# A message-passing layer on one core: the gather of B[dst] and the scatter of edge sums replaced by 0/1 matmuls over a window of 64 nodes

## The chip, the cores and the metric

The kernel runs on one core of a Trainium2 chip. The metric is device time in microseconds (us) of one launch. The program is the same for every run, and its inputs are fixed by a seed.

## The reference

There are N = 6250 nodes with 128 features and E = 100000 edges with 4 attributes. The edges are **sorted by destination**; on average a node has 16 of them.

```python
# x: [6250, 128], src, dst: [100000] (sorted by dst), edge_attr: [100000, 4]
msg_in = concat([x[src], x[dst], edge_attr], axis=1)      # [E, 260]
h = silu(msg_in @ mW1 + mb1)
messages = h @ mW2 + mb2
aggregated = segment_sum(messages, dst, num_segments=N)
u = silu(concat([x, aggregated], axis=1) @ uW1 + ub1)
y = layer_norm(x + u @ uW2 + ub2, ln_g, ln_b)
out = layernorm(x + y)
```

## The kernel before

The linear parts of the edge network are moved to the nodes. With A = x @ mW1a and B = x @ mW1b + mb1, an edge needs silu(A[src] + B[dst] + edge_attr @ mW1e). The second matrix is applied after the sums, because sum(h @ mW2 + mb2) = sum(h) @ mW2 + degree * mb2. All arithmetic is in float32.

The work has three stages.

**Tables (lines 94 to 195).** Nodes lie on 128 partitions, 49 to each. x is loaded, transposed on TensorE in batches of four node tiles, and multiplied to A and B. Both go to tables in DRAM, `tab_a` and `tab_b` (lines 194, 195). Two accumulators in DRAM, `acc`, are filled with zeros by two large DMAs on ScalarE's queue (line 170). ScalarE's queue also issues the weight loads, among them 16 small ones for the block-diagonal edge weights `we` (line 121).

**Edges (lines 198 to 307).** 128 edges make a tile, 4 tiles a group, and there are 196 groups, so 784 tiles. For each tile GpSimd (POOL) issues three indirect DMAs: a gather of A[src] into `ga`, one of B[dst] into `gb` (both line 229), and a scatter that adds 128 rows of 144 numbers to an accumulator (line 292). Gathers run 3 groups ahead. A group's computing is: transposes of the destinations (`pd`, line 254), a 0/1 matrix of equal destinations within a tile (`same`, line 256), three further VectorE operations that find which lane comes first (lines 260 to 268), the edge attributes' part (`pre`, line 272), two additions (lines 276, 277), silu on ScalarE (`h`, line 279), four products of `same` with `h` (`ph`, line 285) and two copies out of PSUM (line 288).

**Node update and the norms (lines 309 to 422).** Per batch of four node tiles, both accumulators are loaded (line 328) and added (line 330), transposed (`ps_s`, `ps_d`, lines 334, 335) and sent through the update network: `ps_a` (343, 344), `ps_u` (349, 352), silu (354), `ps_y` (358). Then the two norms follow in chunks of 7 node tiles (lines 392 to 422).

The order on each engine is not the program's order. A scheduler that runs when the kernel is built places an operation on its engine as soon as its inputs and a free buffer are there by its own reckoning; the buffer counts (`bufs`) bound how far it runs ahead. On each engine the order is then fixed, and semaphores carry the waits.

Of the kernel before, what the change touches and what calls it, by code (L numbers as in the profile page):

```python
# [12 lines left out]
AX = mybir.AxisListType  # L13
PSUM = bass.MemoryType.PSUM
DRAM = bass.MemoryType.DRAM

P = 128
EPS = 1e-5


@with_exitstack
def kernel(
# [30 lines left out]
    """  # L53
# [5 lines left out]
    NP = P * NT  # L59
    G = 4                       # edge tiles in a group  # L60
    C = 16                      # edge tiles whose attributes are transposed together
    ET = -(-E // (P * C)) * C
    NG = ET // G
    W = 144                     # features, degree, and zeros up to a multiple of 64 bytes
    K = 2                       # accumulators that scatters alternate between
    SPARE = NP                  # first spare row
    NA = NP + P
    AHEAD = 3                   # groups that gathers run ahead
# [4 lines left out]
    def load_rows(tile_, src_rows, n_rows, per, split=112):  # L73
        """Rows p * per .. of a [n_rows, ...] array to partition p; the last partition may be short."""
        full = n_rows // per
        for p0, p1 in ((0, min(split, full)), (min(split, full), full)):
            if p1 > p0:
                nc.sync.dma_start(
                    tile_[p0:p1],
                    src_rows[p0 * per : p1 * per].rearrange("(p j) c -> p j c", j=per),  # L80
                )
        rest = n_rows - full * per
        if rest:
            nc.sync.dma_start(
                tile_[full : full + 1, :rest],
                src_rows[full * per : n_rows].rearrange("(p j) c -> p j c", p=1),
            )
# [7 lines left out]
    x_sb = consts.tile([P, NT, H], F32, name="x_sb")  # L95
    last = N // NT
    if N % P or N % NT:
        nc.vector.memset(x_sb[96:P], 0.0)
    load_rows(x_sb, x, N, NT)
# [4 lines left out]

    src_i = consts.tile([P, ET, 1], I32, name="src_i")
    dst_i = consts.tile([P, ET, 1], I32, name="dst_i")
    ea = consts.tile([P, ET, ED], F32, name="ea")
    nc.gpsimd.memset(src_i[96:P], 0)
    nc.gpsimd.memset(dst_i[96:P], N)
    nc.gpsimd.memset(ea[96:P], 0.0)  # L110
    load_rows(src_i, src.rearrange("(e o) -> e o", o=1), E, ET)
    load_rows(dst_i, dst.rearrange("(e o) -> e o", o=1), E, ET)
    load_rows(ea, edge_attr, E, ET)

    # block-diagonal edge weights: row (j, c) holds mW1e[c] in block j
    NB = C // G
    we = consts.tile([C * ED, NB, G * H], F32, name="we")
    nc.vector.memset(we, 0.0)
    for j in range(C):
        b, g = divmod(j, G)  # L120
        nc.scalar.dma_start(we[j * ED : (j + 1) * ED, b, g * H : (g + 1) * H], mW1[2 * H :])

# [15 lines left out]
    ident = consts.tile([P, P], F32, name="ident")  # L138
    make_identity(nc, ident)
    col = consts.tile([P, P], I32, name="col")  # L140
    nc.gpsimd.iota(col, pattern=[[1, P]], base=0, channel_multiplier=-1)
    below = consts.tile([P, P], F32, name="below")      # column < partition
    nc.vector.tensor_scalar(below, col, 0.0, None, op0=OP.is_lt)
    spare_i = consts.tile([P, 1], I32, name="spare_i")
    nc.gpsimd.iota(spare_i, pattern=[[0, 1]], base=SPARE, channel_multiplier=1)
    spare = consts.tile([P, 1], F32, name="spare")
    nc.vector.tensor_copy(spare, spare_i)
# [4 lines left out]
    tab_a = dram.tile([NP, H], F32, name="tab_a")  # L152
    tab_b = dram.tile([NP, H], F32, name="tab_b")
    acc = [dram.tile([NA, W], F32, name=f"acc{k}") for k in range(K)]
    xT = consts.tile([P, NT * P], F32, name="xT")

    def by_node(t):
        return t[:NP].rearrange("(p i) f -> p i f", i=NT)

    def groups(n, g):  # L160
        return [(i, min(g, n - i)) for i in range(0, n, g)]

    with tc.tile_pool(name="tables", bufs=3) as work, tc.tile_pool(
        name="zero", bufs=1
    ) as zpool, tc.tile_pool(name="tables_ps", bufs=2, space=PSUM) as ps:
        NZ = NA * W // P
        zeros = zpool.tile([P, NZ], F32, name="zeros")
        nc.gpsimd.memset(zeros, 0.0)
# [29 lines left out]
    with ExitStack() as edges:  # L198
        idxp = edges.enter_context(tc.tile_pool(name="idxp", bufs=1))
        gath = edges.enter_context(tc.tile_pool(name="gath", bufs=AHEAD + 2))  # L200
# [4 lines left out]
        dst_f = idxp.tile([P, ET], F32, name="dst_f")  # L205
        nc.vector.tensor_copy(dst_f, dst_i.rearrange("p j o -> p (j o)"))
        to_spare = idxp.tile([P, ET], F32, name="to_spare")
        nc.vector.tensor_scalar(to_spare, dst_f, -1.0, spare, op0=OP.mult, op1=OP.add)
        NH = 3
        hbuf = []  # L210
        for i in range(NH):
            h = idxp.tile([P, G, W], F32, name=f"h{i}")
            nc.vector.memset(h[:, :, H:], 0.0)
            nc.vector.memset(h[:, :, H : H + 1], 1.0)
            hbuf.append(h)

        rows = {}

        def gather(g, i):
            if g >= NG:  # L220
                return
            if i == 0:
                rows[g] = (
                    gath.tile([P, G, H], F32, name="ga"),
                    gath.tile([P, G, H], F32, name="gb"),
                )
            j = g * G + i
            for t, tab, idx in zip(rows[g], (tab_a, tab_b), (src_i, dst_i)):
                nc.gpsimd.indirect_dma_start(  # L229
                    out=t[:, i, :],  # L230
                    out_offset=None,
                    in_=tab[:, :],
                    in_offset=bass.IndirectOffsetOnAxis(ap=idx[:, j, :], axis=0),
                )
# [221 lines left out]
```

## Time and profile before

| | |
|---|---|
| Time, median of 3 runs | 3765.49 us (3764.08 to 3770.97) |
| Profiled execution, first to last instruction (span) | 3770.8 us |
| First gather starts | 80.92 us |
| Last scatter starts | 3613.53 us |
| Mean granted TensorE clock | 0.523 of full speed |

No time is listed for the profiled execution apart from its span; the span lies 5.3 us over the median and 0.2 us under the slowest of the three runs, so that span and time are read as one here.

How to read the profile: the engines are PE (TensorE's matmuls), PEld (its weight loads, which overlap PE), DVE (VectorE), ACT (ScalarE), POOL (GpSimd) and SP (SyncE, which only issues DMAs here). A name with q (SPq) is an engine's instruction queue. "out<-in" names tiles of the program. In the timeline the columns are start in us, duration in us, engine, line, operation, tiles, shapes, count, and in brackets the engine's idle time before it and what ended it. A float32 matmul appears as two rows (784 of them at line 285 make x1568), a transpose as one.

### The profile page before, as it was taken

The numbers are of one execution on the slowest core, as the hardware profiler recorded it, in microseconds if no ns is written. First come the engines' busy times: TensorE is split into PE (matmuls) and PEld (weight loads), VectorE is DVE, ScalarE is ACT, GpSimd is POOL, SyncE is SP. The second block draws the span as 40 slices with busy tenths as digits, with TensorE's granted clock in tenths as the row PEclk, the third lists the DMA queues.
The fourth block names the chain that finished last, engine by engine and source line by source line (L and its number), as shares of the span: only waits on it lengthen the run. The fifth ranks groups of instructions, "written<-read, shape, count | busy, mean of one in ns | idle before, by whom it ended". The sixth has DMA issues, their size and how long they took to land.

```text
span 3770.8 us, 14615 instructions
## 1 busy us (share of the span) xinstructions
PE 1171.2 (31%) x3240; PEld 685.3 (18%) x3240; DVE 829.6 (22%) x1701; ACT 363.5 (10%) x793; POOL 2858.9 (76%) x2384
## 2 busy tenths in 40 slices
PE   4332223322332233222332233223322233223261
PEld 3211111111111111111111111111111111111131
DVE  3221121212221222112121222112211212122144
ACT  0100000000000000000000000000000000000024
POOL 2777777777777777777777777777777777777750
PEclk8555555555555555555555555555555555555576
DMA  6222222222222222222222222222222222222231
GB/s 220 47 46 46 46 45 46 46 46 45 46 46 46 45 46 46 46 46 45 46 46 46 46 45 46 45 46 46 46 46 46 45 46 46 46 46 45 46 91 34
DMA packets 174372, 192.16 MB, mean 51 GB/s; under 512 B 39183, under 2 KB 141394, under 8 KB 173774
## 3 DMA queue, kind: packets, MB, share of 16 engines
q0 software_dynamic: 163072, 160.71, 27.1%
q1 hardware_dynamic: 9242, 22.45, 1.9%
q10 hardware_dynamic: 1970, 8.06, 0.6%
q8 instruction: 26, 0.43, 0.1%
q14 instruction: 62, 0.50, 0.0%
HBM read 116.27 MB, written 74.80 MB: 51 GB/s over the span
## 4 chain that ended last, share of the span: by engine, by line
POOL 54%; issue 36%; DMA 4%; PE 2%; DVE 1%; ACT 1%; POOLq 0%; SPq 0%; ACTq 0%; DVEq 0%
POOL acc L292 28%; POOL ga L229 20%; POOL gb L229 6%; DMA ga<-tab_a,src_i 2%; DMA acc<-hs,row 2%; ACT o L415 1%; ACT z L400 0%; DVE st L322 0%; PE ps_y L358 0%; PE ps_u L352 0%; PE ps_a L344 0%; PE ps_a L343 0%; DMA part<-acc 0%; PE ps_u L349 0%; DVE z L407 0%
## 5 line engine op out<-in xcount | busy, mean ns | idle before, releaser
L292 POOL DMA_INDIRECT acc<-hs,row x784 | 1273.5, 1624 | 241.1 <-issue 228.6
L272 PE MATMUL pre<-we,eaT 64*128 64x512 f32 x392 | 403.7, 1132 | 2274.9 <-DVE s L277 2273.7
L229 POOL DMA_INDIRECT ga<-tab_a,src_i x784 | 801.0, 1022 | 307.7 <-issue 238.5
L229 POOL DMA_INDIRECT gb<-tab_b,dst_i x784 | 741.3, 946 | 238.8 <-issue 234.2
L272 PEld LDWEIGHTS pre<-we,eaT 64*128 64x128 f32 x392 | 97.2, 307 | 2352.2 <-DVE s L277 2349.4
L276 DVE TENSOR_TENSOR s<-ga,gb 128x512 f32<-128x512 f32 x196 | 135.8, 693 | 1665.2 <-DMA gb<-tab_b,dst_i 1665.1
L285 PE MATMUL ph<-h,same 128*128 128x144 f32 x1568 | 448.2, 467 | 29.7 <-ACT h L279 29.7
L285 PEld LDWEIGHTS ph<-h,same 128*128 128x128 f32 x1568 | 380.2, 330 | 322.1 <-issue 290.2
L279 ACT ACTIVATE h<-s 128x512 f32<-128x512 f32 x196 | 123.5, 630 | 2585.9 <-DVE s L277 2585.9
L256 DVE TENSOR_TENSOR same<-pd,dst_f 128x512 f32<-128x512 f32 x196 | 135.4, 691 | 835.7 <-PE ph L285 835.7
L254 PE MATMUL pd<-ident,dst_f 128*128 128x128 f32 x784 | 215.1, 430 | 151.7 <-DVE same L256 150.2
L288 ACT COPY hs<-ph 128x288 f32<-128x288 f32 x392 | 156.0, 398 | 556.6 <-PE ph L285 556.6
L254 PEld LDWEIGHTS pd<-ident,dst_f 128*128 128x128 f32 x784 | 138.8, 215 | 225.2 <-DVE same L256 222.6
L260 DVE TENSOR_TENSOR before<-same,below 128x512 f32<-128x512 f32 x196 | 135.5, 692 | 6.5
L262 DVE TENSOR_REDUCE n_before<-before 128x4 f32<-128x512 f32 x196 | 134.3, 685 | 6.5
L277 DVE TENSOR_TENSOR s<-s,pre 128x512 f32<-128x512 f32 x196 | 133.2, 680 | 0.0
L268 DVE TENSOR_TENSOR row<-shift,dst_f 128x4 int32<-128x4 f32 x196 | 32.1, 164 | 269.1 <-DMA acc<-hs,row 269.0
L396 POOL TENSOR_TENSOR xb<-x_sb,b_b 128x896 f32<-128x896 f32 x7 | 16.0, 2301 | 42.4 <-DVE z L408 42.4
L360 POOL TENSOR_TENSOR xu<-x_sb,ub_b 128x512 f32<-128x512 f32 (+1 forms) x13 | 16.0, 1237 | 41.5 <-DVE y L363 39.5
L264 DVE SCALAR_TENSOR_TENSOR shift<-n_before,to_spare 128x4 f32<-128x4 f32 x196 | 32.5, 166 | 6.7
L181 PE MATMUL pab<-w,xT 128*128 128x256 f32 x98 | 25.9, 424 | 11.5 <-DVE tb L191 10.8
L181 PEld LDWEIGHTS pab<-w,xT 128*128 128x128 f32 x98 | 20.4, 214 | 16.0 <-DVE tb L191 11.2
(66 smaller groups left out, 395.5 us busy)
## 6 DMA issues: line engine op xcount, KB each, us to landing
ga<-tab_a,src_i POOLq DMA_INDIRECT x784, 2.6
gb<-tab_b,dst_i POOLq DMA_INDIRECT x784, 2.5
acc<-hs,row POOLq DMA_INDIRECT x784, 3.4
acc<-zeros ACTq DMA_DIRECT2D x2, 3600.0 KB
part<-acc SPq DMA_DIRECT2D x24, 288.0 KB
tab_a<-ta SPq DMA_DIRECT2D x12, 256.0 KB
tab_b<-tb SPq DMA_DIRECT2D x12, 256.0 KB
x_sb<-in_x_dram SPq DMA_DIRECT2D x1, 2744.0 KB
```

Source lines behind the costliest of these rows:

```text
L229: nc.gpsimd.indirect_dma_start(out=t[:, i, :], out_offset=None, in_=tab[:, :], in_offset=bass.IndirectOffsetOnAxis(ap=idx[:, j, :], axis=0),)
L254: nc.tensor.transpose(pd[:, i, :], dst_f[:, j : j + 1].to_broadcast([P, P]), ident)
L256: nc.vector.tensor_tensor(same, pd, dst_f[:, js, None].to_broadcast([P, G, P]), op=OP.is_equal)
L260: nc.vector.tensor_mul(before, same, below[:, None, :].to_broadcast([P, G, P]))
L262: nc.vector.tensor_reduce(n_before, before, AX.X, OP.add)
L272: nc.tensor.matmul(pre.rearrange("p g f -> p (g f)"), eaT, we[:, g % NB, :], start=True, stop=True)
L276: nc.vector.tensor_add(s, ga, gb)
L277: nc.vector.tensor_add(s, s, pre)
L279: nc.scalar.activation(h[:, :, :H], s, AF.Silu)
L285: nc.tensor.matmul(ph[:, i, :], same[:, i0 + i, :], h[:, i0 + i, :], start=True, stop=True)
L288: nc.scalar.copy(hs[:, i0 : i0 + 2, :], ph)
L292: nc.gpsimd.indirect_dma_start(out=acc[(g * G + i) % K][:, :], out_offset=bass.IndirectOffsetOnAxis(ap=row[:, i, :], axis=0), in_=hs[:, i, :],
```

## The change

The edge stage and the storage of the sums are rewritten; the tables and the update network keep their arithmetic.

**Layout.** Node n now lies in tile n // 128 on partition n % 128, so rows of one node (512 bytes) are the pieces in which x, the tables and the output move. An edge group is still 512 edges, but lane c of a group holds edges 4c to 4c + 3. The index lists are loaded flat and turned into that layout by TensorE transposes; a flag `bad_i` is computed that says whether any group's destinations reach beyond 64 nodes from the group's first.

**Edges.** Only A[src] is gathered: 4 indirect DMAs a group, 8 groups ahead. Since the edges are sorted, a group's destinations lie in a window of W = 64 nodes that starts at its first destination, `bases[g]`. SyncE loads the 64 rows of B in that window, four times side by side, into partitions 0 to 63 of a tile `m`, whose partitions 64 to 79 hold the edge weights. A stationary tile `st` holds a 0/1 matrix of destination against window row in partitions 0 to 63, and the transposed edge attributes in partitions 64 to 79. One matmul for each tile then gives B[dst] + edge_attr @ mW1e. The sums are made the same way: `oh`, 128 edges by 64 window rows, is multiplied with `h` and accumulated over the 4 tiles in PSUM, for the features (`pw`) and the degrees (`pd`), and VectorE adds both to `acc` and `deg` in SBUF, at a column that is read from a register. The registers are loaded 14 at a time on SP and on DVE.

**Update.** `acc` already lies transposed in SBUF, so the loads, the addition of the two accumulators and the transposes go; the work pool has 2 buffers instead of 3. At the end all engines read the flag, and behind a branch stand a general path (the old method in a loop) and a second update.

```diff
-        for k in range(K):
-            nc.scalar.dma_start(acc[k].rearrange("(p i) w -> p (i w)", p=P), zeros)
...
+    NM = 4
+    mv = []
+    for k in range(NM):
+        t = consts.tile([K1, G, H], F32, name=f"mv{k}")
+        nc.vector.memset(t[W:K1], 0.0)
+        for i in range(G):
+            nc.scalar.dma_start(t[W + i * ED : W + (i + 1) * ED, i, :], mW1[2 * H :])
+        mv.append(t)
...
-        gath = edges.enter_context(tc.tile_pool(name="gath", bufs=AHEAD + 2))
+        gath = edges.enter_context(tc.tile_pool(name="gath", bufs=AHEAD + 3))
+        chunk = edges.enter_context(tc.tile_pool(name="chunk", bufs=2))
         work = edges.enter_context(tc.tile_pool(name="edge", bufs=3))
         ps = edges.enter_context(tc.tile_pool(name="edge_ps", bufs=2, space=PSUM))
         ps1 = edges.enter_context(tc.tile_pool(name="edge_ps1", bufs=1, space=PSUM))
...
+        def fetch(g):
             if g >= NG:
                 return
+            rows[g] = gath.tile([P, G, H], F32, name="ga")
             for i in range(G):
+                gather(rows[g][:, i, :], tab_a, src_i[:, g, i : i + 1])
+
+        def load_chunk(g):
+            e0 = g * GE
+            n = min(CH * GE, E - e0)
+            t = chunk.tile([W, CH * GE], I32, name="dst_w")
...
+            nc.sync.dma_start(
+                t[:, :n], dst[e0 : e0 + n].rearrange("(o e) -> o e", o=1).to_broadcast([W, n])
+            )
...
+        def load_bases(g):
+            _, vals = nc.values_load_multi_w_load_instructions(
+                base_i[0:1, g : g + RB],
+                engines=(ENG.SP, ENG.DVE),
...
+        def first(g):
+
+            if g % CH == 0:
+                load_chunk(g)
+            if g % RB == 0:
+                load_bases(g)
+            m = mv[g % NM]
+            nc.sync.dma_start(
+                m[:W], tab_b[bass.ds(bases[g], W), :][:, None, :].to_broadcast([W, G, H])
+            )
+            st = work.tile([K1, G, P], F32, name="st")
+            k = g % CH
+            nc.vector.tensor_scalar(
+                st[:W],
+                dst_w[g // CH][:, k * GE : (k + 1) * GE].rearrange("w (c i) -> w i c", i=G),
+                base_p[:W, g : g + 1],
+                None,
+                op0=OP.is_equal,
+            )
+            pe = ps1.tile([EK, P], F32, name="pe")
+            nc.tensor.transpose(pe, ea[:, g, :], ident)
+            nc.scalar.copy(st[W:K1], pe[:, None, :].to_broadcast([EK, G, P]))
+            pre = ps.tile([P, G, H], F32, name="pre")
+            for i in range(G):
+                nc.tensor.matmul(pre[:, i, :], st[:, i, :], m[:, i, :], start=True, stop=True)
+            oh = work.tile([P, G, W], F32, name="oh")
             nc.vector.tensor_tensor(
+                oh,
+                w_row[:, None, :].to_broadcast([P, G, W]),
+                rel[:, g, :, None].to_broadcast([P, G, W]),
+                op=OP.is_equal,
+            )
+            s = work.tile([P, G, H], F32, name="s")
+            nc.vector.tensor_add(s, rows.pop(g), pre)
+            h = work.tile([P, G, H], F32, name="h")
+            nc.scalar.activation(h, s, AF.Silu)
+            return h, oh
+
+        def second(g, h, oh):
+            pw = ps.tile([P, W], F32, name="pw")
+            pd = ps1.tile([1, W], F32, name="pd")
+            for i in range(G):
+                nc.tensor.matmul(pw, h[:, i, :], oh[:, i, :], start=i == 0, stop=i == G - 1)
+            for i in range(G):
+                nc.tensor.matmul(pd, ones[:, 0:1], oh[:, i, :], start=i == 0, stop=i == G - 1)
+            for to, of in ((acc, pw), (deg, pd)):
+                at = to[:, bass.ds(bases[g], W)]
+                nc.vector.tensor_add(at, at, of)
+
+        for g in range(AHEAD):
+            fetch(g)
+        held = None
+        for g in range(NG + 1):
+            fetch(g + AHEAD)
+            now = first(g) if g < NG else None
+            if held is not None:
+                second(g - 1, *held)
+            held = now
...
+            for i0, n in groups(NT, BG):
+                cols = slice(i0 * P, (i0 + n) * P)
+                ps_a = ps.tile([P, BG * P], F32, name="ps_a")
+                nc.tensor.matmul(ps_a[:, : n * P], w2, acc[:, cols], start=True, stop=False)
+                nc.tensor.matmul(ps_a[:, : n * P], mb2_row, deg[:, cols], start=False, stop=True)
...
+    update("", acc, deg)
+
+
+    bad = nc.values_load(bad_i[0:1, 0:1], min_val=0, max_val=1,
+                         skip_runtime_bounds_check_because="the result of a comparison")
+    with tc.If(bad > 0):
+        general(ctx, tc, tab_a, tab_b, src_i, dst_f, ea, p_col, ident, mW1, acc, deg, N)
+        update("_g", acc, deg)
```

The function `general` loops over the 196 groups. In each turn it gathers A[src] and B[dst] by eight indirect DMAs, computes `pre`, `s` and `h`, and for each of the 4 tiles builds `same`, the row list and the summed rows, and scatters them with an accumulating DMA; all its tiles have one buffer.

More of the change, by code (lines that the diff above doesn't have):

```diff
@@ L13 @@
 AX = mybir.AxisListType
+ENG = mybir.EngineType
 PSUM = bass.MemoryType.PSUM
@@ L18 @@
 EPS = 1e-5
+IN_RANGE = "indices of nodes, which the reference takes to be in range"
 @with_exitstack
@@ L58, with groups @@
     NT = -(-N // P)
-    NP = P * NT
+    NP = NT * P
     G = 4
[L61 to L68, printed above, removed]
+    GE = G * P
+    NG = -(-E // GE)
+    assert NG % 2 == 0 and NG // 2 <= P
+    W = 64
+    NW = NP + W
+    EK = G * ED
+    K1 = W + EK
+    CH = 4
+    RB = 14
+    AHEAD = 8
+    assert NG % CH == 0 and NG % RB == 0
     consts = ctx.enter_context(tc.tile_pool(name="consts", bufs=1))
     dram = ctx.enter_context(tc.tile_pool(name="dram", bufs=1, space=DRAM))
[L73 to L87, printed above, removed]
+    def groups(n, g):
+        return [(i, min(g, n - i)) for i in range(0, n, g)]
     def bcast(name, row):
@@ L172 @@
+    lists_scope.close()
+    with tc.tile_pool(name="tables", bufs=3) as work, tc.tile_pool(
+        name="tables_ps", bufs=2, space=PSUM
+    ) as ps:
+        zeros = work.tile([W, H], F32, name="zeros")
+        nc.vector.memset(zeros, 0.0)
+        nc.sync.dma_start(tab_b[NP:NW], zeros)
         for i0, n in groups(NT, 4):
@@ L217 @@
-        rows = {}
-        def gather(g, i):
+        rows, dst_w, bases = {}, {}, {}
+        def fetch(g):
             if g >= NG:
                 return
[L222 to L225, printed above, removed]
-                )
[L227 to L233, printed above, removed]
-                )
@@ new lines, in general @@
+        for i in range(NP // P):
+            part = keep.tile([P, WR], F32, name="part")
+            nc.sync.dma_start(part, sums[i * P : (i + 1) * P])
+            p_s = ps.tile([P, P], F32, name="p_s")
+            nc.tensor.transpose(p_s, part[:, :H], ident)
+            nc.vector.tensor_copy(acc[:, i * P : (i + 1) * P], p_s)
+            p_d = ps.tile([1, P], F32, name="p_d")
+            nc.tensor.transpose(p_d, part[:, H : H + 1], ident)
+            nc.vector.tensor_copy(deg[:, i * P : (i + 1) * P], p_d)
```

490 lines of the change are left out of this document (285 added, 205 removed).

## The prediction, made before the changed kernel was run

> **What bounds the kernel now.** I read the page's busy shares and its chain of work first, then the groups of instructions, then the timeline of a stretch in the middle.
>
> ```profile
> span 3770.8 us, 14615 instructions
> PE 1171.2 (31%) x3240; PEld 685.3 (18%) x3240; DVE 829.6 (22%) x1701; ACT 363.5 (10%) x793; POOL 2858.9 (76%) x2384
> ...
> POOL 54%; issue 36%; DMA 4%; PE 2%; DVE 1%; ACT 1%; POOLq 0%; SPq 0%; ACTq 0%; DVEq 0%
> ...
> L292 POOL DMA_INDIRECT acc<-hs,row x784 | 1273.5, 1624 | 241.1 <-issue 228.6
> ...
> L229 POOL DMA_INDIRECT ga<-tab_a,src_i x784 | 801.0, 1022 | 307.7 <-issue 238.5
> L229 POOL DMA_INDIRECT gb<-tab_b,dst_i x784 | 741.3, 946 | 238.8 <-issue 234.2
> ```
>
> POOL is busy for 76% of the span, and most of the rest is "issue", 0.30 us ahead of each instruction (238.5 / 784). POOL and issue make up 90% of the chain that ended last. So POOL writes descriptors without a break, 3 x 784 instructions. The timeline shows the period:
>
> ```profile
> 2007.14 1.63 POOL L292 DMA_INDIRECT acc<-hs,row  x1 [0.30 <-issue]
> ...
> 2025.11 1.63 POOL L292 DMA_INDIRECT acc<-hs,row  x1 [0.30 <-issue]
> ```
>
> These two scatters stand four scatters apart, one group: 17.97 us. By the groups it is 4 x (1.624 + 1.022 + 0.946 + 3 x 0.30) = 18.0 us; 196 groups take 3522 of the 3770.8 us.
>
> **The change, part by part.** **POOL** loses 8 of its 12 instructions of a group and keeps 4 gathers. Ahead of the first scatter gathers ran alone:
>
> ```profile
> 82.51 0.97 POOL L229 DMA_INDIRECT ga<-tab_a,src_i  x1 [0.30 <-issue]
> ...
> 100.05 0.94 POOL L229 DMA_INDIRECT gb<-tab_b,dst_i  x1 [0.30 <-issue]
> ...
> 2004.03 0.69 DVE L276 TENSOR_TENSOR s<-ga,gb 128x512 f32<-128x512 f32 x1 [8.16 <-DMA gb<-tab_b,dst_i]
> 2004.41 1.18 POOL L229 DMA_INDIRECT ga<-tab_a,src_i  x1 [0.30 <-issue]
> ```
>
> From the first to the second are 14 steps, 17.54 / 14 = 1.25 us each, so 5.0 us a group. A gather that begins while DVE works took 1.18 instead of 0.94; DVE will work more densely around the gathers, and if all four were so slow, a group would be 4 x (1.18 + 0.30) = 5.9. I take one in four: 5.2.
>
> **PE** is next, and it runs at half clock in this stage (0.50 in the windows further down).
>
> ```profile
> L285 PE MATMUL ph<-h,same 128*128 128x144 f32 x1568 | 448.2, 467 | 29.7 <-ACT h L279 29.7
> ...
> 2008.91 1.94 PEld L285 LDWEIGHTS ph<-h,same 128*128 128x128 f32 x8 [1.50 <-issue]
> 2008.91 2.29 PE L285 MATMUL ph<-h,same 128*128 128x144 f32 x8
> ...
> 3621.81 0.42 PE L335 MATMUL ps_d<-ident,part 128*1 128x128 f32 x1
> ...
> 3622.02 0.42 PE L334 MATMUL ps_s<-ident,part 128*128 128x128 f32 x1
> ```
>
> A float32 matmul is two rows (784 matmuls, x1568). Eight rows of 144 columns take 2.29 us, at most 0.29 each; two transposes of 128 columns start 0.21 apart. Per group the new PE work is: `pre`, 8 rows of 128 columns at 0.21 to 0.29, taken 0.25: 2.0 us. `pw`, 8 rows of 64 columns: the columns alone would be half of 0.21, but each matmul loads new weights of 128 columns, and eight such loads took 1.94, 0.24 each; so 0.85 to 1.94, taken 1.9, since the load is the nearer row. `pd`, 8 rows of 64 columns with weights of one column: 8 x 0.11 = 0.9. The transpose `pe`: 0.2. Together **5.0 us** (3.9 to 5.4). PE goes from 5.4 busy in 18 us to nearly saturated, level with POOL.
>
> **The other engines** are hidden by these two.
>
> ```profile
> L276 DVE TENSOR_TENSOR s<-ga,gb 128x512 f32<-128x512 f32 x196 | 135.8, 693 | 1665.2 <-DMA gb<-tab_b,dst_i 1665.1
> ...
> L279 ACT ACTIVATE h<-s 128x512 f32<-128x512 f32 x196 | 123.5, 630 | 2585.9 <-DVE s L277 2585.9
> ...
> L264 DVE SCALAR_TENSOR_TENSOR shift<-n_before,to_spare 128x4 f32<-128x4 f32 x196 | 32.5, 166 | 6.7
> ...
> q0 software_dynamic: 163072, 160.71, 27.1%
> ...
> ga<-tab_a,src_i POOLq DMA_INDIRECT x784, 2.6
> ...
> acc<-zeros ACTq DMA_DIRECT2D x2, 3600.0 KB
> ...
> L328 SPq DMA_DIRECT2D part<-acc x26: 319/320/617, 3617.1 to 3673.4; - x26
> ```
>
> DVE: `st` and `s` have 512 columns (0.69 each), `oh` 256 (0.35), the two additions into `acc` and `deg` are small (0.17 each): 2.1 us. ACT: a copy of 512 columns (0.58 by the `ta` row below) and silu (0.63): 1.2 us. DMA: before, 784 x 384 row moves took 27.1% of 16 engines, 16 x 3770.8 x 0.271 / 301056 = 0.054 us a row on one engine. Now a group has 512 gathered rows and 256 rows of the B window, 768 x 0.054 / 16 = 2.6 us; the destinations' broadcast and the attributes (136 KB, at 160.71 MB in those 16350 engine-us) add 0.9. That is 3.5 of 5.2, hidden while gathers run 8 groups ahead and windows 4. SP issues about 1.5 DMAs a group at 0.32 us.
>
> The **register loads** have no row: 14 on SP and 14 on DVE for every 14 groups, and behind them in DVE's queue stands `st`, for which PE's `pre` waits. From below they cost nothing (DVE has 3 us to spare in each group, and `st` has three buffers). From above each would be a full landing of a gather (2.6 us, the `ga` row): 36 us in 14 groups, 2.6 a group. The nearest row is an issued DMA, 0.32: 4.5 us in 14 groups, of which I leave half uncovered: 0.15 a group. The Trainium skill ("Runtime: NRT & Kernel Launch", Instruction fetch mechanics) gives about 200 ns for a register load, which speaks against the change by 2.8 us in 14 groups; no run here shows one yet.
>
> With two stations at 5.0 and 5.2 us that pass work through two or three buffers, I allow 0.2 for their waiting on each other: 5.2 + 0.2 + 0.15 = **5.55 us a group**, 196 x 5.55 = 1088 us.
>
> **Before the edges.**
>
> ```profile
> 9.67 19.80 ACTq L121 DMA_DIRECT2D we<-in_L_gnn_mW_dram  x16
> ...
> 55.52 0.58 ACT L190 COPY ta<-pab 128x512 f32<-128x512 f32 x1 [12.70 <-DMA tab_a<-ta]
> ...
> 64.49 3.69 PE L181 MATMUL pab<-w,xT 128*128 128x256 f32 x16 [0.33 <-ACT eaT L246]
> ...
> 69.49 0.89 PE L181 MATMUL pab<-w,xT 128*128 128x256 f32 x3 [0.33 <-ACT eaT L246]
> ...
> 80.92 1.29 POOL L229 DMA_INDIRECT ga<-tab_a,src_i  x1 [69.17 <-DMA tab_b<-tb]
> ```
>
> The zeros go (2 x 3600 KB, the `acc` row above), and with them the wait of 12.70 us for a table write. ACT still issues 16 small weight loads (19.8 us) and now half of x, so its first `ta` may come at 40. Two table batches take 69.49 - 64.49 = 5.0, thirteen 33, and the last write lands in about a gather's 2.6: first gather at 75 (60 to 90), and 10 more until the first group is through. The turning of the index lists lies on DVE and PE while x loads.
>
> **After the edges.**
>
> ```profile
> 3613.53 1.56 POOL L292 DMA_INDIRECT acc<-hs,row  x1 [0.30 <-issue]
> ...
> 3620.73 0.76 DVE L330 TENSOR_TENSOR part<-part,part 128x576 f32<-128x576 f32 x1 [27.73 <-DMA part<-acc]
> ...
> 3665.95 1.12 PE L344 MATMUL ps_a<-dT,mb_row 1*128 1x512 f32 x2
> ...
> 3667.00 0.60 PE L335 MATMUL ps_d<-ident,part 128*1 128x128 f32 x4
> ...
> 3671.68 1.12 PE L344 MATMUL ps_a<-dT,mb_row 1*128 1x512 f32 x2
> ```
>
> The last scatter starts 157.3 us before the end. Its landing, the load and the addition go, 3613.5 to 3621.5: 8 us. A batch takes 3671.68 - 3665.95 = 5.73 with PE full; the transposes go, `ps_d` 0.60 and `ps_s` as long, overlapping, so about 0.9 of it: 13 x 0.9 = 12. That leaves 138; with 2 buffers instead of 3, 140. The flag's read and the jump have no row: nothing to 30 us (a landing of 2.6 on each engine and a code fetch, one after another); I take 7.
>
> **Sum:** 75 + 10 + 1088 + 140 + 7 = **1320 us**. It is made against the span, 3770.8, which lies 0.1% over the median; that is inside the range.
>
> **The rivals.** **POOL alone bounds.** What speaks for it is that PE can double its clock:
>
> ```profile
> 58.00:62.00 4.00, 4.00 (x11) 3.19 (x10) 0.73 (x2) 0.58 (x1) 0.00 (x0) 0.50 0.63 241
> 62.00:66.00 4.00, 3.67 (x21) 3.07 (x21) 1.96 (x4) 0.84 (x2) 0.00 (x0) 0.99 0.59 219
> 2007.00:2011.00 4.00, 4.00 (x10) 2.35 (x10) 0.00 (x0) 0.98 (x2) 3.25 (x3) 0.50 0.36 56
> 3627.00:3631.00 4.00, 4.00 (x21) 2.36 (x20) 1.98 (x3) 1.27 (x2) 1.53 (x1) 1.00 0.67 171
> ```
>
> (The last three columns are the granted clock, DMA share and GB/s.) In the tables 4 us without a break at 0.50 were followed by 0.99, and the update holds 1.00. At full clock PE would need 2.5 us, and a group is POOL's 5.0 to 5.2: 75 + 10 + 196 x 5.1 + 140 + 7 = 1232. Against it: in the edge stage 4.00 of 4.00 us busy stayed at 0.50, where half of the matmuls use 64 of 128 rows; the new loop's `pre` uses 80 rows, `pd` one column, and PE must wait for POOL. The Trainium skill ("TensorE: Matmul & The Clock Gate", Part 1) says that some 3.4 us of sustained matmuls open the gate; by that rule the time is the 1232 of this rival, and the window at 2007 does not agree. Chance 0.22.
>
> **A serial chain bounds.** In the program's order DVE adds `deg` of group g - 1 before it makes `st` of g + 1, so that a group would be `st` 0.69 + `pre` 2.0 + `pw` 1.9 + `pd` 0.9 + addition 0.17 + four hand-overs of about 0.1 = 6.1, and the register loads, uncovered, 0.3: 6.4, or 1486 in all. Against it:
>
> ```profile
> L256 DVE TENSOR_TENSOR same<-pd,dst_f 128x512 f32<-128x512 f32 x196 | 135.4, 691 | 835.7 <-PE ph L285 835.7
> ```
>
> DVE's `same` waits for `ph`, the reader of its buffer three groups back: the scheduler does run ahead as far as buffers allow. But two of the new links have one buffer. Chance 0.25.
>
> **Registers or window loads cost a landing each**: 2.6 a group more, 5.2 + 2.6 = 7.8, 1761. Chance 0.06.
>
> **The branch is taken (slower than before).** If one group's 512 sorted destinations reached over more than 64 nodes, `general` would run behind all of the above: POOL's 8 gathers and 4 scatters again, 196 x 17.97 = 3522 at least, with one buffer and so nothing overlapped, and a second update of 140: 1320 + 3522 + 140 = 4982 or more. 512 edges at 16 a node are 32 nodes, and the widest group of the reference's inputs reaches 36. Chance 0.01.
>
> **How the numbers follow.** Forecast 0.46 (its own range 1250 to 1420), POOL alone 0.22, serial chain 0.25, landings 0.06, branch 0.01. The range runs from 1200 (first gather at 65, 196 x 5.0 = 980, tail 145) to 1600 (a chain of 7 us a group); it leaves out the landings, the branch and a little of either flank. 0.2% is about what a measurement of this kernel can tell from no change; every case but the branch is faster by far more: faster 0.98, same 0.01, slower 0.01.
>
> **What would show it.** POOL: 784 gathers about 1.3 us apart in the edge stage, DMA scatters gone. PE: busy over 85% there at a clock near 0.50, `pw` rows about 0.24 apart. If the clock reads 1.00 and POOL shows only issue gaps, POOL alone decides. If POOL waits for DVE's `s` and PE waits for `st`, it is the chain. If DVE or SP stands still for microseconds every 14th group, it is the registers. The forecast is wrong if a group takes under 5.1 or over 6 us, or if the first gather starts outside 60 to 90.

## The result and the profile after

The changed kernel takes **1566.15 us** (median of 5 runs, 1553.23 to 1572.34), the kernel before 3768.41: a ratio of 0.4153, 95% interval 0.4136 to 0.4170. The profiled execution took 1553.23 us with a span of 1551.4. The forecast was 1320, in a range of 1200 to 1600.

The page of the changed kernel, its busy shares, the chain that ended last and the groups that answer to the forecast's terms:

```profile
span 1551.4 us, 16190 instructions
PE 1099.7 (71%) x5268; PEld 880.8 (57%) x5268; DVE 491.2 (32%) x1296; ACT 300.5 (19%) x535; POOL 860.7 (55%) x817
...
PE 61%; another core or an unknown queue 16%; issue 8%; ACT 6%; DVE 4%; DMA 3%; SPq 1%; POOL 0%; DVEq 0%; ACTq 0%; POOLq 0%
...
L261 POOL DMA_INDIRECT ga<-tab_a,src_i x784 | 817.1, 1042 | 518.0 <-issue 214.5
L348 PE MATMUL pre<-mv,st 80*128 80x128 f32 x1568 | 407.0, 441 | 132.3 <-ACT st L345 90.8
...
L345 ACT COPY st<-pe 16x512 f32<-16x512 f32 x196 | 112.5, 574 | 796.8 <-remote 409.8
...
L371 DVE TENSOR_TENSOR deg<-deg,pd 1x64 f32 x196 | 40.6, 207 | 185.7 <-remote 133.7
```

PE has taken the place of POOL at the head of the chain, as a kernel whose edge stage lost its scatters should show. Two things do not fit. PE is busy for only 71%, and 16% of the chain, some 250 us, belong to an "unknown queue". The same shows at the right end of the last two rows: ACT's copy into `st` and DVE's addition into `deg` sat idle for 409.8 and 133.7 us and the profile names no instruction that released them ("remote"), although, apart from its own engine, each waits for nothing but PE's `pe` and `pd`.

By the timeline the parts of the time are: first `s` at 109.2, last addition into `acc` at 1405.1, end at 1551.4. So the edges took 1296 us, 6.61 a group; 85 + 1088 + 147 were forecast for the three parts, 109 + 1296 + 146 came. The error sits in the edges.

The timeline shows what such a "remote" wait is. One group of the changed kernel (start, duration, then in brackets the idle time before and its releaser):

```profile
813.78 0.80 PE L368 MATMUL pd<-oh,ones 128*1 128x64 f32 x6
...
814.51 0.38 PE L344 MATMUL pe<-ident,ea 128*16 128x128 f32 x1
...
818.34 0.21 DVE L371 TENSOR_TENSOR deg<-deg,pd 1x64 f32 x1 [3.76 <-remote]
...
818.61 0.37 PE L368 MATMUL pd<-oh,ones 128*1 128x64 f32 x2 [3.71 <-DVE deg L371]
...
819.09 0.57 ACT L345 COPY st<-pe 16x512 f32<-16x512 f32 x1 [8.54 <-remote]
```

PE's `pd` rows are over at 814.58, DVE is free, and `deg` still starts only at 818.34; then PE waits for `deg`. PE's signal before that start was recorded at 818.32, 3.7 us behind the matmul. Nothing else was missing: by the trace the matmuls had run, and their **signals came late**. This happens once in almost every block of four groups, at the place where PE has nothing else to do until `deg` is through. At the start it is worse: from 133 to 173 PE did almost nothing while POOL's gathers went on (windows further down).

### The profile page after: what moved, and what is told of

It is laid out like the page before. It is cut to its first block, busy times and chain, and to the rows that moved or that the text cites. A ratio compares the mean times of both kernels' runs of the same rounds, so it can differ in the third digit from the quotient of the medians.

```text
span 1551.4 us, 16190 instructions
## 1 busy us (share of the span) xinstructions
PE 1099.7 (71%) x5268; PEld 880.8 (57%) x5268; DVE 491.2 (32%) x1296; ACT 300.5 (19%) x535; POOL 860.7 (55%) x817
## 4 chain that ended last, share of the span: by engine, by line
PE 61%; another core or an unknown queue 16%; issue 8%; ACT 6%; DVE 4%; DMA 3%; SPq 1%; POOL 0%; DVEq 0%; ACTq 0%; POOLq 0%
PE pre L348 23%; PE pw L366 19%; PE pd L368 10%; PE pe L344 3%; ACT st L345 3%; DMA dst_l<-in_dst_dram 2%; PE pab L241 1%; ACT o L470 1%; ACT z L455 1%; PE ps_a L403 1%; PE ps_y L417 1%; PE ps_u L407 1%; PE ps_a L402 1%; PE ps_u L408 1%
## 5 line engine op out<-in xcount | busy, mean ns | idle before, releaser
L348 PE MATMUL pre<-mv,st 80*128 80x128 f32 x1568 | 407.0, 441 | 132.3 <-ACT st L345 90.8
L348 PEld LDWEIGHTS pre<-mv,st 80*128 80x128 f32 x1568 | 349.2, 327 | 181.8 <-ACT st L345 110.2
L366 PE MATMUL pw<-oh,h 128*128 128x64 f32 x1568 | 363.1, 413 | 13.4 <-issue 13.3
L366 PEld LDWEIGHTS pw<-oh,h 128*128 128x128 f32 x1568 | 353.9, 330 | 25.4 <-issue 24.3
L368 PE MATMUL pd<-oh,ones 128*1 128x64 f32 x1568 | 228.4, 300 | 163.6 <-DVE deg L371 111.3
L357 DVE TENSOR_TENSOR s<-ga,pre 128x512 f32<-128x512 f32 x196 | 134.7, 687 | 424.5 <-PE pre L348 264.6
L345 ACT COPY st<-pe 16x512 f32<-16x512 f32 x196 | 112.5, 574 | 796.8 <-remote 409.8
L368 PEld LDWEIGHTS pd<-oh,ones 128*1 128x1 f32 x1568 | 117.2, 104 | 237.5 <-DVE deg L371 129.3
L336 DVE TENSOR_SCALAR st<-dst_w,base_p 64x512 f32<-64x512 int32 x196 | 129.8, 662 | 4.0 <-ACT h L359 2.8
L371 DVE TENSOR_TENSOR deg<-deg,pd 1x64 f32 x196 | 40.6, 207 | 185.7 <-remote 133.7
L350 DVE TENSOR_TENSOR oh<-w_row,rel 128x256 f32<-128x256 f32 x196 | 79.7, 407 | 18.1 <-issue 18.1
```

The source lines that it names most:

```text
L336: nc.vector.tensor_scalar(st[:W], dst_w[g // CH][:, k * GE : (k + 1) * GE].rearrange("w (c i) -> w i c", i=G), base_p[:W, g : g + 1], None ...
L345: nc.scalar.copy(st[W:K1], pe[:, None, :].to_broadcast([EK, G, P]))
L348: nc.tensor.matmul(pre[:, i, :], st[:, i, :], m[:, i, :], start=True, stop=True)
L350: nc.vector.tensor_tensor(oh, w_row[:, None, :].to_broadcast([P, G, W]), rel[:, g, :, None].to_broadcast([P, G, W]), op=OP.is_equal,)
L357: nc.vector.tensor_add(s, rows.pop(g), pre)
L366: nc.tensor.matmul(pw, h[:, i, :], oh[:, i, :], start=i == 0, stop=i == G - 1)
```

## Experiments

Twelve experiments in four sets, each set on one chip; the chip of set 0, the first measurement, is not on record. One table first, since the sets matter more than the kernels. Late signals are those recorded more than 0.5 us after the end of the matmul that sends them, out of all recorded; three at the ends of the program are late in every run. Where records are missing, the matmul of a signal has to be guessed, so the larger counts are good to some 7%. The next column is how many of the gathers' landing signals (16 for each gather) stand in the trace. "A group" is the time from the first `s` to the last addition into `acc`, over 196. The time is the median of five runs in set 0, a single run for all of set 1, for registers_twice and for no_gathers, and the median of four elsewhere. The other columns come from one execution, in two_banks_again the quickest of the four (1496.78), in two_banks_third the slowest (1603.55).

```
run               set   time us   late / recorded   landings recorded   a group
changed kernel     0     1566.15    153 / 729        3177 of 12544        6.61
no_degrees         1     1258.92      3 / 676       12407 of 12544        5.13
two_banks          1     1275.52      3 / 868       12410 of 12544        5.21
one_gather         1     1302.71      3 / 872        3126 of  3136        5.36
two_chunks         1     1309.40      3 / 871       12522 of 12544        5.37
after_again        2     1570.19    125 / 716        3318 of 12544        6.64
two_banks_again    2     1536.23    317 / 729        2498 of 12544        6.36
registers_twice    2     1575.60    158 / 705        3258 of 12544        6.75
after_third        3     1305.52      3 / 873       12458 of 12544        5.35
no_gathers         3     1304.03      3 / 872        none                 5.36
tables_first       3     1290.26      3 / 849       12351 of 12544        5.28
two_banks_third    4     1567.82    348 / 756        2299 of 12544        6.87
free_act           4     1579.98    323 / 731        3000 of 12544        6.78
```

**Set 1: what makes the gap?** The theories were a hand-over over a single PSUM buffer (A), signals held back while gathers run (B), and the chunk load of destinations (C).

no_degrees:

```
-            for i in range(G):
-                nc.tensor.matmul(pd, ones[:, 0:1], oh[:, i, :], start=i == 0, stop=i == G - 1)
-            for to, of in ((acc, pw), (deg, pd)):
+            for to, of in ((acc, pw),):
```

> Leaves out the four pd matmuls of a group and the addition into deg (deg stays 0). Theory A (single hand-over): the gap of about 4 us in every fourth group is the exchange between PE and DVE over the one pd buffer, pd to deg to the next pd; without pd it goes, PE needs pre 2.1 + pw 1.8 + pe 0.4 = 4.3 us a group, POOL's four gathers of 1.25 bound at 5.1, and the time is 1566 - 196 x 1.5 = about 1270. Theory B (PE's signals come late while gathers run, whatever the matmul): the gaps stay and stand before another DVE instruction that waits for PE (acc or s); only PE's 0.9 us a group goes, and the time is 1566 - 196 x 0.9 = about 1390.

two_banks:

```
-        ps1 = edges.enter_context(tc.tile_pool(name="edge_ps1", bufs=1, space=PSUM))
+        ps1 = edges.enter_context(tc.tile_pool(name="edge_ps1", bufs=2, space=PSUM))
```

> pe and pd get two PSUM buffers each instead of one. Theory A: the gaps of every fourth group (some 176 us in all) shrink or go, 1390 to 1450. Theory B: the order of the work changes a little, the late signals stay, 1530 to 1580.

one_gather:

```
-            for i in range(G):
-                gather(rows[g][:, i, :], tab_a, src_i[:, g, i : i + 1])
+            gather(rows[g], tab_a, src_i[:, g, 0:1])
...
-            nc.vector.tensor_add(s, rows.pop(g), pre)
+            nc.vector.tensor_add(s, rows.pop(g)[:, None, :].to_broadcast([P, G, H]), pre)
```

> Leaves out three of a group's four gathers; s adds the one gathered row to all four lanes (the sums are of other rows). Theory A: POOL is not what PE waits for, the exchange between PE and DVE stays as it is, 1540 to 1566. Theory B: with a quarter of the gathers in flight the gaps go in most groups; a group takes the 5.36 us of the last twelve groups, after POOL's end, and the edges begin without their 75 us stop: 109 + 196 x 5.36 + 146 = about 1310. If POOL's rate itself were the bound (5.0 to 5.2 a group), it would be near 1310 too, but POOL waits for DVE in the trace of after.

two_chunks:

```
+            if g < 2 * CH:
+                t = chunk.tile([W, CH * GE], I32, name="dst_w")
+                nc.sync.dma_start(
...
+            else:
+                t = dst_w[g // CH - 2]
```

> Loads the broadcast destinations of the first two chunks of four groups only; later groups compare against these (other nodes are summed). Theory C (the gap follows the 512 KB broadcast load that comes once in four groups): the gaps go, 1350 to 1400. Theories A and B as stated so far: no change but for a little DMA traffic, 1540 to 1570.

Measured: 1259, 1276, 1303 and 1309. no_degrees came near the 1270 of A, one_gather near the 1310 of B, and two_banks and two_chunks lower than any theory had asked. Read one by one against 1566, each edit would have found the cause. Three exclusive theories cannot all be right: four edits with nothing in common had each run without the late signals, so the unedited kernel was missing from the set.

**Set 2: the unedited kernel.** after_again is the changed kernel, unaltered.

> The changed kernel once more, unaltered. Four edits that have little in common have each taken away all of the late signals of PE, and 250 to 300 us with them. Theory D (the late signals belong to the executions measured first, not to the program): no late signals now, PE bounds a group at 5.36 us, 109 + 196 x 5.36 + 146 = about 1305. Theory E (they belong to the program, by a meeting of chunk load, gathers and single PSUM buffers that each edit breaks up): 1550 to 1575 again, with a gap of 3 to 4 us in every fourth group.

> The kernel with two PSUM buffers for pe and pd once more, for a ratio against the kernel before and beside after_again on one chip. Both theories: 1265 to 1285. Under theory D it is then 2 to 3% faster than after_again, by the hand-overs over one buffer alone; under theory E 18%.

registers_twice (the value loads of a block are written a second time, their results unused):

```
+            nc.values_load_multi_w_load_instructions(base_i[0:1, g : g + RB], engines=(ENG.SP, ENG.DVE), ...)
             for k, v in enumerate(vals):
                 bases[g + k] = v
```

> Every 14 register loads on SP and on DVE are issued twice (3.0 us more on each, 14 times, 42 us in all). If they stand on the path, as the forecast's 0.15 us a group has it for half of them, the time rises by 20 to 42 us over after_again; if PE's queued work and the three st buffers cover them, by less than 8. Under theory E the shifted order may also take the late signals away: about 1305.

Measured: after_again 1570.19, ratio 0.4171 (0.4150 to 0.4191), the first result again. That would have spoken for theory E, but two_banks, the same text as in set 1, now took 1536 (ratio 0.4068, 0.4037 to 0.4100) instead of 1276, with 317 late signals instead of 3. The kernel was the same and the late signals were not: they did not come from the buffers. The size of the gain is rough, since the four runs of two_banks_again spread from 1497 to 1565 and those of after_again from 1555 to 1584.

registers_twice took 1575.60, but it did not do what it was meant to do. Its trace has as many register loads as the unedited kernel, 14 on DVE and 14 on SP, one for each block of 14 groups:

```profile
L314 DVEq TENSOR_LOAD <-base_i x14: 1314/3019/3185, 93.6 to 1324.0; - x14
```

The second loads, whose results nothing reads, are not in the program that ran. So this is in effect one more run of the changed kernel, and it gives no price of a register load.

**Set 3: by chip, or by program?**

> The changed kernel unaltered, a third time. So far the four runs on one chip show no late PE signal in any kernel and the three on another chip show them in all. Theory D, now by chip: this run gives either 1300 to 1310 with no PE signal over 0.5 us late (109 + 196 x 5.36 + 146), or 1555 to 1585 with some 125 late ones and 9 us a group in the first 20, and the other kernels of this set go the same way. Theory E (the program's own order): 1555 to 1585, whatever the others do.

no_gathers:

```
-            for i in range(G):
-                gather(rows[g][:, i, :], tab_a, src_i[:, g, i : i + 1])
...
-            nc.vector.tensor_add(s, rows.pop(g), pre)
+            nc.vector.tensor_add(s, x_sb[:, 0:G, :], pre)
```

> Leaves out all gathers; s adds rows of x instead. On a chip without late signals PE alone bounds and a group stays at 5.3 to 5.4 us: 1290 to 1305, which shows that POOL is not the bound of the changed kernel. On a chip with them: if gathers in flight hold PE's signals back, they are gone and the time is the same 1290 to 1305; if they come from anything else (chunk loads, the recording), over 1450.

tables_first (two_banks, and the block that turns the index lists stands behind the block that builds the tables):

> Two PSUM buffers for pe and pd, and the tables built before the index lists are turned, so that PE and DVE work on x while the lists load. The first gather comes at 80 to 90 instead of 100, the rest as with two buffers: 1255 to 1268 on a chip without late signals, 1480 to 1550 on one with them. If the lists' landing at 44 us, the turning behind the tables and their chain set the first gather anyway, no gain over 1275.

Measured: after_third **1305.52** (four runs, 1303.82 to 1306.82), ratio **0.3458** (0.3452 to 0.3463). This is the program that took 1566 and 1570. The same place of its timeline:

```profile
805.31 0.80 PE L368 MATMUL pd<-oh,ones 128*1 128x64 f32 x6
...
806.04 0.38 PE L344 MATMUL pe<-ident,ea 128*16 128x128 f32 x1
806.15 0.21 DVE L371 TENSOR_TENSOR deg<-deg,pd 1x64 f32 x1
...
806.41 0.37 PE L368 MATMUL pd<-oh,ones 128*1 128x64 f32 x2
806.51 0.57 ACT L345 COPY st<-pe 16x512 f32<-16x512 f32 x1 [4.43 <-PE pe L344]
```

`deg` follows `pd` within 0.04 us, the copy is released by `pe` by name, and there is no "remote". The page of after_third has the same matmuls and the same work of PE, without the unknown queue:

```profile
span 1302.7 us, 16190 instructions
PE 1095.7 (84%) x5268; PEld 879.5 (68%) x5268; DVE 490.9 (38%) x1296; ACT 299.7 (23%) x535; POOL 852.2 (65%) x817
...
PE 77%; ACT 7%; DMA 5%; POOL 4%; DVE 3%; issue 3%; SPq 1%; ACTq 0%; DVEq 0%; POOLq 0%
```

Windows of the changed kernel as first measured (length, then busy time of PE, PE's weight loads, DVE, ACT and POOL, then granted clock, DMA share and GB/s):

```profile
133.00:173.00 40.00, 0.14 (x1) 0.00 (x0) 1.16 (x3) 0.00 (x0) 29.33 (x32) 0.50 0.18 52
...
300.00:900.00 600.00, 473.16 (x2326) 389.53 (x2325) 188.35 (x465) 112.70 (x187) 389.92 (x375) 0.50 0.32 82
```

The same windows of after_third:

```profile
133.00:173.00 40.00, 35.70 (x174) 29.18 (x173) 13.79 (x36) 8.41 (x14) 30.86 (x31) 0.50 0.42 99
...
300.00:900.00 600.00, 569.94 (x2803) 469.34 (x2803) 226.11 (x560) 134.61 (x224) 463.47 (x449) 0.50 0.40 99
```

PE is busy for 570 of 600 us where signals are prompt, and for 473 where they are late; in the stop at the start POOL is busy almost as long as in the other run (29.3 against 30.9 us), and all engines that wait for PE stand. no_gathers, without any gather, takes 1304.03, as long as after_third with 784:

```profile
300.00:900.00 600.00, 565.65 (x2783) 465.57 (x2782) 225.00 (x559) 134.31 (x224) 0.00 (x0) 0.50 0.18 49
```

So where signals are prompt the gathers cost this kernel nothing; the loop through PE bounds it, and POOL does not. tables_first took 1290.26, ratio 0.3419 (0.3411 to 0.3428): the quickest version with an interval, 1.2% under after_third in the same set. Its first gather came at 100.5 all the same, so what it gained came from the edges (5.28 a group instead of 5.35), where it has the second PSUM buffers.

**Set 4: a ratio for two_banks, and an earlier start.**

> Two PSUM buffers for pe and pd, for a ratio in several rounds. On a chip without late signals: 1270 to 1280, 2 to 3% under the changed kernel's 1305 by the hand-over over one buffer (PE's waits for the copy st and for deg, some 50 us in all); on one with them 1490 to 1565.

free_act (tables_first, and these loads leave ACT's queue):

```
-            nc.scalar.dma_start(t[W + i * ED : W + (i + 1) * ED, i, :], mW1[2 * H :])
+            nc.gpsimd.dma_start(t[W + i * ED : W + (i + 1) * ED, i, :], mW1[2 * H :])
...
-    nc.scalar.dma_start(w2, mW2)
+    nc.gpsimd.dma_start(w2, mW2)
```

> Two PSUM buffers, tables before lists, and the 16 small loads into mv and the eight of late-needed weights issued by POOL, which is idle there, instead of ACT. If the first gather came at 100 instead of 75 because ACT issued small loads until 56 us and made its first table copy only then, the tables now follow x's landing at 45 to 48: first gather at 70 to 80, and 1250 to 1268 on a chip without late signals. If the lists or the chain of table batches set it, it stays at 95 to 100 and the time at 1275 to 1290. On a chip with late signals 30 us under the other kernel or the same as it.

Measured: 1567.82 and 1579.98, with 348 and 323 late signals, on the very chip that had given set 1 without one. So theory D falls in its form by chip as well: neither the program nor the chip alone decides, but something that held for each whole set. For two_banks a ratio without late signals is missing; its single run of 1275.52 against after_third's 1305.52 stands in different sets.

What free_act was for can still be read, since the stage before the edges has no late signals. Where the changed kernel's first gather comes from:

```profile
46.14 9.63 ACTq L146 DMA_DIRECT2D mv<-in_L_gnn_mW_dram  x16
57.58 1.28 ACT L250 ACT_TABLE_LOAD   x1 [57.58 <-DVE bad_i L223]
62.62 0.59 ACT L250 COPY ta<-pab 128x512 f32<-128x512 f32 x1 [3.75 <-PE pab L241]
...
43.99 0.69 DVE L192 CAST tf<-dst_l 98x1024 f32<-98x1024 int32 x1 [17.80 <-DMA dst_l<-in_dst_dram]
...
57.37 0.13 DVE L223 TENSOR_SCALAR bad_i<-farthest 1x1 int32<-1x1 f32 x1
...
56.90 1.97 PE L235 MATMUL pt<-ident,x_sb 128*128 128x128 f32 x8 [0.73 <-DVE farthest L222]
...
101.17 1.12 POOL L261 DMA_INDIRECT ga<-tab_a,src_i  x1 [87.04 <-DMA ea<-in_edge_attr_dram]
```

The list of destinations lands at 44, its turning and the flag run until 57.5, and PE begins with the tables only at 56.9, behind the last step but one of them. ACT issues small loads until 56 besides. tables_first took away the first of these and met the second; here is its longest wait of ACT before the tables, and then the end of that stage in free_act, which took away both:

```profile
ACT L212 <- DMA mv<-in_L_gnn_mW_dram: 55.2, 1, 55.2
```

```profile
78.26 0.27 ACT L212 COPY ta<-pab 128x128 f32<-128x128 f32 x1 [0.63 <-PE pab L203]
...
96.01 0.13 DVE L255 TENSOR_SCALAR bad_i<-farthest 1x1 int32<-1x1 f32 x1
...
97.08 1.04 POOL L262 DMA_INDIRECT ga<-tab_a,src_i  x1 [66.19 <-ACT st L346]
```

The last table copy ends at 78.5 (the changed kernel issues its last table write at 98.5), and the first gather still comes at 97.1. POOL stood at a wait for DVE until the flag `bad_i` was done (96.1), and then, by the row above, for ACT's copies into `st`. So in that order of the program the gathers' first instruction stands behind the whole list stage, the flag included. The gathers need only the source list, and that is there early: in the changed kernel DVE casts it at 25.5, but the step that makes `src_i` of it stands behind the cast of the destinations and starts at 44.8:

```profile
25.49 0.69 DVE L192 CAST tf<-src_l 98x1024 f32<-98x1024 int32 x1 [21.96 <-DMA src_l<-in_src_dram]
...
44.76 1.56 DVE L201 CAST src_i<-pt 128x392 int32<-128x392 f32 x2
```

Neither moving that step ahead nor leaving the flag for later was tried.

## Why the prediction was right or wrong

- **The changed kernel itself: right, with help from luck.** In set 3 it takes 1305.5 where 1320 was forecast (1.1% too high), inside the forecast's own 1250 to 1420. The parts are 108 to the first `s`, 1049 for the edges and 145 behind them, against 85 + 1088 + 147: the start came 23 us later, the edges were 39 us shorter, and the two errors hide each other.
- **The result of 1566: not foreseen.** Between the edges of the first measurement (1296) and those of set 3 (1049) lie 247 us, for the same program; they come and go with the late signals of PE, which no step of the forecast contains. The step that failed by that measurement is the one that says "I allow 0.2 for their waiting on each other": by the windows above PE stood idle for 127 of 600 us, 1.4 us a group. By the forecast's own test (a group over 6 us) it is wrong there, 6.61. The range of 1200 to 1600 holds both values, but 1566 only because the rival with a chain had stretched it that far; the mechanism of that rival was not at work, so this is luck.
- **Bound of the edges: right.** "PE goes from 5.4 busy in 18 us to nearly saturated, level with POOL" came so. PE's terms can be read from the starts of the rows in after_third:

```profile
800.15 1.01 PE L368 MATMUL pd<-oh,ones 128*1 128x64 f32 x8
801.09 0.38 PE L344 MATMUL pe<-ident,ea 128*16 128x128 f32 x1
801.27 1.81 PE L366 MATMUL pw<-oh,h 128*128 128x64 f32 x8
803.01 0.37 PE L368 MATMUL pd<-oh,ones 128*1 128x64 f32 x2
803.31 2.08 PE L348 MATMUL pre<-mv,st 80*128 80x128 f32 x8
805.31 0.80 PE L368 MATMUL pd<-oh,ones 128*1 128x64 f32 x6
```

  From each start to the next, `pd` takes 0.94 (0.9 forecast), `pe` 0.18 (0.2), `pw` 1.74 (1.9) and `pre` 2.00 (2.0), 4.86 in all where 5.0 was forecast. The durations in the rows overlap, so their sum would be too long. By busy time PE needs 570 us for the 112 groups in the 600 us, 5.09 each. POOL's 5.2 was right too: without `pd`, no_degrees needs 5.13 a group, DVE's `s` waits for gathers there, and POOL's row gives 4 x (0.980 + 0.30) = 5.12:

```profile
L261 POOL DMA_INDIRECT ga<-tab_a,src_i x784 | 768.0, 980 | 324.1 <-issue 222.6
```

  So the two are level, as forecast. The later one is PE, with the wait that follows.
- **Waits of the two stations (0.2) and registers (0.15): near in size, not between these stations.** In after_third PE is idle for 30 of the 600 us, 0.27 a group, and all of it stands in front of `pre` (total, times, longest):

```profile
PE pre L348 <- ACT st L345: 30.1, 56, 0.7
```

  PE waits for ACT's copy out of the one `pe` buffer, not for POOL: no_gathers has 30 us of the same wait. The **register loads** were priced too high. One instruction loads 14 registers, and it takes 1.3 to 3.2 us on DVE, 0.09 to 0.23 a register, not 0.32. The Trainium skill ("Runtime: NRT & Kernel Launch", Instruction fetch mechanics) gives about 200 ns for one; the longer loads here agree with that, the shorter take half.

```profile
L314 DVEq TENSOR_LOAD <-base_i x14: 1314/2998/3193, 96.7 to 1304.7; - x14
```

  What a load costs the loop shows best in no_gathers, where the groups are most regular. By the starts of `s`, the two groups in which the load falls take 11.2 us together, and other pairs 10.7 to 10.8: about 0.5 in 14 groups, 0.03 a group.
- **First gather at 75: wrong**, 101, outside the 60 to 90 that the forecast named as its own test. The step was "The turning of the index lists lies on DVE and PE while x loads": the list landed only at 44, and the tables stood behind it and behind ACT's loads. It cost 23 us of the start.
- **Tail and flag, 140 + 7: right**, 146. **Clock at 0.50: right**; it stayed there for the whole edge stage. The rule of the Trainium skill ("TensorE: Matmul & The Clock Gate", Part 1) that some 3.4 us of sustained matmuls open the gate is not borne out here: PE was busy for 95% of 600 us in after_third, with stretches of 10 us that have no gap, and the clock read 0.50. So the rival "POOL alone" had its condition fail.
- **The serial chain** (1486) came nearest to 1566 in time, and it would be easy to call it right. It was not: the same program with the same single buffers takes 5.35 a group when signals are prompt, not 6.4. What is left of the chain there is the wait of 0.27 above. A second buffer took 0.08 a group off in the same set (tables_first, 5.28) and 0.14 in two_banks (5.21), but that is a single run in another set, and its clock was higher (0.53 in mean from 300 to 900 against 0.50). There DVE's `s` waits for gathers for 266 of the 600 us, so POOL comes next as the bound. What the single buffers cost when signals are late is not settled: in set 2 two buffers were worth 2.5% (0.4068 against 0.4171), in set 4 the same kernel took 1567.82 with no unedited kernel beside it.

**What stays open** is what makes the signals late. The runs show: it held for whole sets, with both kinds of set on one chip; the kernel before took 3764 to 3781 in all of them; where PE's signals are late, 74 to 82% of the gathers' landing signals are missing from the trace as well, and at most 2% where they are prompt; and in the last groups of the changed kernel, behind the last gather, nothing is late (the last twelve take 5.3 us each). Records of the other engines are missing too: as first measured, the trace has 984 signals of DVE where its 1290 instructions that send one ran, and 338 of ACT's 461; after_third has all of both. The one trace of the kernel before has all 37632 landings of its 2352 indirect DMAs. Whether the recording of signals itself holds them back, or both have one cause, these runs cannot tell: every time here is that of a recorded execution. Two rivals were never tested where they count. No kernel without gathers, and none without the chunk loads, was measured in a set with late signals, although in the first measurement one gap comes with almost every four groups, as a chunk load does. Set 1 does not rule these two out, since its unedited kernel would have had no late signals either, as far as sets tell.

## What to carry to other kernels

Before a gap is explained, run the unedited kernel beside the edits: three theories were each "confirmed" here by a set in which the gap did not exist. A wait whose releaser the profile cannot name, behind an instruction that is long done, is a sign to ask whether the trace is complete, not a place for a story about buffers. And when an engine at 95% bounds, the edit that pays is the one that takes rows from it or lets it run ahead: here a second PSUM buffer for `pe` and `pd`, measured together with a new order of the tables, took off 1.2%. Last, before a price is read from an added instruction, find it in the trace: the second register loads, whose results nothing read, never ran.

## What the runs showed of the hardware

A matmul's end in the trace and the moment at which other engines see its signal can lie far apart. The worst place is at the start of the changed kernel's edges, here by PE's timeline:

```profile
131.17 1.97 PE L366 MATMUL pw<-oh,h 128*128 128x64 f32 x8 [11.44 <-issue]
...
182.72 0.42 PE L344 MATMUL pe<-ident,ea 128*16 128x128 f32 x1
```

and by DVE's:

```profile
186.20 0.22 DVE L371 TENSOR_TENSOR acc<-acc,pw 128x64 f32 x1 [12.09 <-remote]
```

The first row is the `pw` of the third group, which ends at 133.1; the last is the addition of that `pw`, 53 us later, and DVE had been idle for 12.09 us before it. Few of PE's signals stand in the trace between them, at 156.54, 173.34 and 177.74. Then, at 186.18 to 186.43, four were recorded within 0.25 us, 3 us after the last matmul that sends one (`pe`, the second row, ends at 183.14). So these matmuls had been done before, as far as the modelled ends of matmuls tell. The Trainium skill ("Perfetto Trace Analysis", Tensor Engine Instruction) sets the acknowledged write, the signal and its being visible apart as steps of their own, but gives no time for the last.

The clock does open for this loop, but no length of busy time that these runs show decides it. In two_banks, 12 us busy without a break were followed by 9 us at full clock, while 59 us without a break, earlier in the same run, stayed at half clock. It closed again once PE, at full clock, had gaps; in them DVE's `s` waited for gathers (13.0 us from 534 to 555):

```profile
368.50:427.50 59.00, 59.00 (x297) 49.80 (x297) 22.29 (x55) 13.53 (x23) 44.98 (x47) 0.50 0.42 103
...
522.00:534.00 12.00, 12.00 (x67) 10.48 (x65) 3.64 (x10) 3.02 (x6) 9.26 (x10) 0.52 0.48 113
534.00:543.00 9.00, 6.12 (x52) 4.92 (x52) 4.33 (x13) 3.16 (x6) 6.87 (x8) 1.00 0.35 87
543.00:555.00 12.00, 9.09 (x50) 7.50 (x50) 3.64 (x10) 2.06 (x4) 9.01 (x10) 0.53 0.48 119
```
